# Conditional weights: masking, their layout and the counts' bank in a two-stage expert kernel on one Trainium2 core

## The chip, the cores and the metric

The kernel runs on one NeuronCore of one Trainium2 chip. The metric is device microseconds (us) of one execution. The kernel before took 288.45 us, the median of three runs (288.25 to 288.47).

## The reference, cut to what matters

Stage one (conditional weights): each of 128 batches mixes eight masked weight matrices with its own eight condition values, and its 32 tokens are multiplied by the mixed matrix. Stage two (experts): each batch takes the two experts with the largest condition values, and a shared MLP is added. Both stages are residual.

```python
masked_w = weight * mask[None, :, :]                     # weight (8, 128, 128), mask (128, 128)
w_bot = jnp.einsum('bg,got->bot', y, masked_w)           # y = cond_8 (128, 8)
x = x + jnp.einsum('bnt,bot->bno', x, w_bot) + bias      # x (128, 32, 128)

rw = jax.nn.softmax(cond_8); w, sel = jax.lax.top_k(rw, 2); w = w / w.sum(-1, keepdims=True)
# each selected expert e of batch b adds w * (gelu(x @ gate[e]) * (x @ up[e])) @ down[e]
# the shared MLP (128 -> 512 -> 128) adds the same form for every token
x = x + experts(x) + shared_mlp(x)
```

## The kernel before, in words

The features stand on the 128 partitions, the 4096 tokens (128 batches of 32) along the free axis, in eight tiles of 512 tokens (`x_sb`, `x1`, `acc`, `outT`). The order of all instructions is the order in which the program writes them: the scheduling is manual, and each engine runs its own list in that order. Waits follow from what is read and written, and from when a buffer of a pool comes free.

**Loads.** ScalarE's queue loads the condition (`cond_sb`, L86) and one half of the eight weight matrices; SyncE's queue loads the other half (L92), the mask (L94), two token tiles, the bias, the shared MLP and the other six token tiles. Expert weights follow on SyncE's queue once the routing knows the experts.

**Conditional weights.** `cond_rep` (L213) repeats each batch's eight values, TensorE transposes it into `ps_y` (L225), and `spread_cond` (L232) multiplies that by `own4`, a 0/1 pattern, into `yd`. After the transpose TensorE runs three idle products (`warm_up`, L130). The masked weights `mw` are made by four products (L248): for each half of the output features, VectorE does the first four matrices and GpSimd the other four. The output stands in the order (output feature, matrix), so an engine that runs over the features writes one value in every eight. `transpose_weights` (L256) transposes eight blocks of 128x128 on TensorE into four banks of PSUM, the first four blocks from the first half of `mw`, and ScalarE and VectorE copy them to `wT` (L269).

**Units.** A unit (`make_weights`, L279) makes the mixed weights of 32 batches for half of the output features: 16 matmuls into four banks (L286), then two copies on ScalarE and two on VectorE into `W` (L300, L302). There are eight units; three are made before the loop, and two in each of the first two rounds, one in the third. A round (L686) takes two token tiles: `apply_weights` (L305, tile `pz`, copied to `z` by ScalarE), then some routing steps (`advance`), then its units, then `finish_cond` (L324: four transposes to `pt`, and VectorE adds bias and residual into `x1`; GpSimd copies `x1` to `acc`).

**PSUM.** There are eight banks in three pools: three for tag `g`, three for `u`, two for `acc`. In stage one, `bank` (L274) goes through the pools in a fixed cycle, and so every further call of it moves all later tiles along that cycle. A tile takes a bank of its pool that is free, or waits for the readers of an older one.

**Routing.** `routing` (L357) is a chain of small VectorE instructions on the condition that ranks the experts, counts how many batches chose each (`ps_n`, two small matmuls), and assigns tiles of tokens to experts. It is cut in steps with `yield`; `advance(n)` first writes the matmuls that are due and then up to n steps, ending early at a `ROUND`. The counts' bank is drawn at L376 in the first round; its matmuls come at the start of the second round's `advance`, and the copy out of it (L405) comes in a later step, between that round's two units. The slots' matmuls (`ps_i`, `ps_w`, drawn at L487) end the chain, in the middle of the shared MLP.

**MLPs.** Expert and shared tiles run through one pipeline (L587): `pg` and `pu` products, gelu on ScalarE (L565), product on VectorE (L567), and one group later the down product `ps_out` (L552 for all). Two shared tiles run first, then 45 expert tiles with four sets of weight buffers, then the other shared tiles.

Of the kernel before, what the change touches and what calls it, by code (L numbers as in the profile page):

```python
# [10 lines left out]
F32 = mybir.dt.float32  # L11
# [19 lines left out]
def kernel(  # L31
# [16 lines left out]
    nc = tc.nc  # L48
# [38 lines left out]
    mask_sb = const.tile([P, P], F32, name="mask_sb")  # L87
    GQ = G // 2
    w0_sb = []
    for q, engine in enumerate((nc.sync, nc.scalar)):  # L90
        wq = const.tile([P, GQ, P], F32, name=f"w0_{q}", tag=f"w0_{q}")
        engine.dma_start(out=wq, in_=w0T[:, ts(q, GQ), :])  # L92
        w0_sb.append(wq)
    nc.sync.dma_start(out=mask_sb, in_=maskT)  # L94
    x_sb = []
# [32 lines left out]
    def warm_up(n):  # L128
# [5 lines left out]
    nc.scalar.activation(table, ones[:, 0:1], AF.Exp)  # L134

    R = P // G
    own = const.tile([P, R], F32, name="own")
    nc.gpsimd.affine_select(
        out=own,
        in_=ones[:, 0:R],  # L140
        pattern=[[-G, R]],
        base=0,
        channel_multiplier=1,
        compare_op=ALU.is_ge,
        fill=0.0,
    )
    nc.gpsimd.affine_select(
        out=own,
        in_=own,
        pattern=[[G, R]],  # L150
        base=G - 1,
        channel_multiplier=-1,
        compare_op=ALU.is_ge,
        fill=0.0,
    )

# [13 lines left out]
    for e in range(1, E):  # L170
# [34 lines left out]
    W = const.tile([P, B, P], F32, name="W")  # L205

    own4 = const.tile([P, OQ], F32, name="own4")
    nc.vector.tensor_reduce(
        own4, own.rearrange("p (j o) -> p o j", o=OQ), AX.X, ALU.add
    )  # L210

    cond_rep = const.tile([B, P // G, G], F32, name="cond_rep")
    nc.vector.tensor_copy(  # L213
        cond_rep, cond_sb.unsqueeze(1).to_broadcast([B, P // G, G])
    )
# [9 lines left out]
    nc.tensor.transpose(  # L225
        ps_y[:, 0:B], cond_rep.rearrange("b r g -> b (r g)"), ident
    )
# [15 lines left out]

    mw = const.tile([P, P, G], F32, name="mw")
    OH = QB * OB
    for half in range(P // OH):
        for q, engine in enumerate((nc.vector, nc.gpsimd)):
            engine.tensor_tensor(  # L248
                mw[:, ts(half, OH), ts(q, GQ)].rearrange("p o g -> p g o"),
                w0_sb[q][:, :, ts(half, OH)],  # L250
                mask_sb[:, ts(half, OH)].unsqueeze(1).to_broadcast([P, GQ, OH]),
                ALU.mult,
            )
    wT = const.tile([P, NQ, P], F32, name="wT")

    def transpose_weights():  # L256
        TQ = QB // 2
        for i in range(NQ // TQ):
            pool, tag = (ps_u, "u") if i % 2 else (ps_g, "g")
            pt = pool.tile([P, TQ * P], F32, name="pt", tag=tag)  # L260
            for k in range(TQ):
                q = i * TQ + k
                nc.tensor.transpose(  # L263
                    pt[:, ts(k, P)],
                    mw[:, ts(q, OB), :].rearrange("p o g -> p (o g)"),
                    ident,
                )
            copy = nc.vector.tensor_copy if i % 2 else nc.scalar.copy
            copy(wT[:, ts(i, TQ), :].rearrange("p q t -> p (q t)"), pt)  # L269
        spread_cond(NB, B - NB)  # L270
# [3 lines left out]
    def bank(name):  # L274

        pool, tag = {"g": (ps_g, "g"), "u": (ps_u, "u"), "o": (ps_o, "acc")}[next(ring)]
        return pool.tile([P, TB], F32, name=name, tag=tag)
# [66 lines left out]

    def tensor_later(*args, **kwargs):
        due.append((args, kwargs))

    def advance(n):

        for args, kwargs in due:  # L350
            nc.tensor.matmul(*args, **kwargs)  # L351
        due.clear()
        for _ in range(n):
            if next(steps, ROUND) is ROUND:
                break

    def routing():  # L357
# [17 lines left out]

        ps_n = bank("ps_n")  # L376
        tensor_later(ps_n[:, 0:E], ones_h, chosen, start=True, stop=True)
        tensor_later(ps_n[:, E : 2 * E], before_h, chosen, start=True, stop=True)
        ex_sum = small.tile([B, 1], F32, name="ex_sum")
# [23 lines left out]
        yield ROUND  # L403
        np_sb = small.tile([P, 2 * E], F32, name="np_sb")
        nc.vector.tensor_copy(np_sb, ps_n[:, 0 : 2 * E])  # L405
        of_expert, so_far = np_sb[:, 0:E], np_sb[:, E : 2 * E]
# [79 lines left out]

        ps_i = ps_g.tile([P, TB], F32, name="ps_i", tag="g")  # L487
        ps_w = ps_u.tile([P, TB], F32, name="ps_w", tag="u")
        for k in range(2):
# [17 lines left out]
            else:  # L507
# [5 lines left out]
                nc.vector.tensor_tensor(both_hot, hot, hot_0, ALU.add)  # L513
                tensor_later(ps_i[:, 0:NS], batch_h, both_hot, start=True, stop=True)
                tensor_later(ps_w[:, 0:NS], ones, hot_w, start=True, stop=True)
            yield
        yield ROUND

        for n, i, c, s in ((NE, 0, 0, S), (NE2, NE, NE * S, S2)):
# [166 lines left out]
    for i in range(LAST + 1):  # L686
# [4 lines left out]
        for _ in units[0:2]:  # L691
            weights()
            if i == 1:
                advance(1)
        if i == LAST:
# [109 lines left out]
```

## Time and profile before

| What | Value |
|---|---|
| median of three runs | 288.45 us |
| profiled execution, its own time | 288.74 us |
| its span, first to last instruction | 287.0 us |
| TensorE busy | 281.3 us, 98% |
| VectorE busy | 166.4 us, 58% |
| ScalarE busy | 79.0 us, 28% |
| GpSimd busy | 49.9 us, 17% |
| granted TensorE clock | 0.999 |
| DMA, mean over the span | 146 GB/s |

By stages of the span: 0 to 7.7 us are loads, set-up and the transposes of the weights (TensorE busy 6.11 us of 7.70); 7.7 to 35 us are the eight units and the four rounds (26.63 of 27.30); 35 to 50.4 us the first shared tiles (15.40 of 15.40); 50.4 to 220 us mostly the experts (169.60 of 169.60); the rest is the late shared tiles (63.58 of 67.00). Matmuls overlap in the records, so busy time counts a TensorE that has something in flight. A busy TensorE is not one at its peak, but where it has no gap, no other engine sets the time.

### The profile page before, as it was taken

To read this page: it belongs to the slowest core of one execution; us is meant where nothing else is said; L and a number is where in the kernel's file an instruction comes from. 1 tells how busy PE (TensorE), PEld (TensorE's weight loads), DVE (VectorE), ACT (ScalarE), POOL (GpSimd) and SP (SyncE) were. 2 spreads that over 40 slices of the span, in tenths; PEclk is the share of its full clock that TensorE was granted. 3 is DMA by queue.
4 is the path that set the end of the run, shared out by engine and by line. 5 is a ranking of instruction groups with operands and counts; after the bars stand their busy time and mean duration, and the time that the engine had idled before them with its cause. 6 is when DMAs were issued, how large, how long until landed. Compare 5 with 4: busy or idle time off the path is not lost.

```text
span 287.0 us, 12878 instructions
## 1 busy us (share of the span) xinstructions
PE 281.3 (98%) x5096; PEld 211.5 (74%) x5096; DVE 166.4 (58%) x473; ACT 79.0 (28%) x149; POOL 49.9 (17%) x289
## 2 busy tenths in 40 slices
PE   7999999999999999999999999999999999999995
PEld 6977644687788878888889999999997444444443
DVE  4889782366656566756665666666666432333232
ACT  5665322222222222222222222222222122221220
POOL 5002204122222122222222211312200000000000
PEclk9999999999999999999999999999999999999999
DMA  7800390266668667687667767777620200100001
GB/s 193 294 5 3 99 328 15 74 205 188 205 190 251 210 205 220 179 270 204 184 201 242 214 202 206 224 220 228 204 61 2 74 37 0 39 37 0 37 37 46
DMA packets 40770, 41.86 MB, mean 146 GB/s; under 512 B 2816, under 2 KB 26752, under 8 KB 40704
## 3 DMA queue, kind: packets, MB, share of 16 engines
q1 hardware_dynamic: 40272, 40.64, 46.3%
q8 instruction: 42, 0.69, 1.0%
q10 hardware_dynamic: 432, 0.33, 0.3%
q14 instruction: 24, 0.20, 0.2%
HBM read 38.87 MB, written 2.10 MB: 143 GB/s over the span
## 4 chain that ended last, share of the span: by engine, by line
PE 97%; DMA 1%; issue 0%; DVE 0%; ACT 0%
PE pg L552 30%; PE ps_out L552 29%; PE pu L552 29%; PE w L286 3%; PE pz L311 3%; PE pt L328 1%; DMA cond_sb<-in_cond_dram 1%; PE pt L263 1%; PE warm L130 0%; ACT W L302 0%; PE ps_w L351 0%; PE ps_y L225 0%; DVE o L622 0%; DVE cond_rep L213 0%; PE ps_n L351 0%
## 5 line engine op out<-in xcount | busy, mean ns | idle before, releaser
L567 DVE TENSOR_TENSOR h<-ge,pu 128x384 f32<-128x384 f32 (+1 forms) x117 | 69.3, 592 | 77.8 <-PE pu L552 77.7
L565 ACT ACTIVATE ge<-pg 128x384 f32<-128x384 f32 (+1 forms) x117 | 61.4, 525 | 187.2 <-PE pg L552 183.3
L662 DVE SCALAR_TENSOR_TENSOR acc<-ps_out,slot_w,acc 128x32 f32 x260 | 65.2, 251 | 30.0 <-DVE h L567 19.5
L552 PE MATMUL ps_out<-h,wd 128*32 128x192 f32 (+1 forms) x1440 | 74.2, 320 | 0.0
L552 PE MATMUL pg<-xg,wg 128*32 128x192 f32 (+1 forms) x1440 | 74.0, 320 | 0.0
L552 PE MATMUL pu<-xg,wu 128*32 128x192 f32 (+1 forms) x1440 | 73.9, 320 | 0.0
L657 POOL COPY xg<-x 128x32 f32 x260 | 42.0, 210 | 132.2 <-PE pu L552 122.5
L552 PEld LDWEIGHTS pg<-xg,wg 128*32 128x32 f32 x1440 | 50.8, 110 | 8.0 <-issue 1.7
L552 PEld LDWEIGHTS ps_out<-h,wd 128*32 128x32 f32 x1440 | 50.9, 110 | 7.2 <-DVE acc L662 0.8
L552 PEld LDWEIGHTS pu<-xg,wu 128*32 128x32 f32 x1440 | 51.0, 110 | 6.4
L552 PE MATMUL pg<-x,swg 128*128 128x512 f32 x64 | 33.0, 597 | 0.0
L552 PE MATMUL pu<-x,swu 128*128 128x512 f32 x64 | 32.7, 592 | 0.0
L552 PE MATMUL ps_out<-h,swd 128*128 128x512 f32 (+2 forms) x72 | 32.5, 546 | 0.0
L552 PEld LDWEIGHTS ps_out<-h,swd 128*128 128x128 f32 x72 | 13.3, 190 | 15.2 <-issue 13.5
L552 PEld LDWEIGHTS pu<-x,swu 128*128 128x128 f32 x64 | 12.2, 190 | 15.3 <-issue 15.1
L552 PEld LDWEIGHTS pg<-x,swg 128*128 128x128 f32 x64 | 11.7, 190 | 12.8 <-issue 12.0
L300 DVE COPY W<-w 128x512 f32<-128x512 f32 x16 | 10.1, 684 | 1.4 <-PE w L286 1.4
L286 PE MATMUL w<-yd,wT 32*128 32x128 f32 x256 | 10.1, 284 | 0.6 <-ACT W L302 0.5
L286 PEld LDWEIGHTS w<-yd,wT 32*128 32x128 f32 x256 | 8.9, 186 | 1.6 <-issue 0.7
L302 ACT COPY W<-w 128x512 f32<-128x512 f32 x16 | 8.5, 592 | 3.6 <-PE w L286 3.6
L333 POOL COPY acc<-x 128x512 f32<-128x512 f32 x6 | 3.7, 613 | 25.9 <-DVE x L329 25.8
L311 PE MATMUL pz<-W,xin 128*32 128x128 f32 x256 | 7.8, 274 | 0.1
(96 smaller groups left out, 70.0 us busy)
## 6 DMA issues: line engine op xcount, KB each, us to landing
wg<-in_gate_dram SPq DMA_DIRECT2D x45, 256.0 KB, 3.5
wu<-in_up_dram SPq DMA_DIRECT2D x45, 256.0 KB, 3.9
wd<-in_down_dram SPq DMA_DIRECT2D x45, 256.0 KB, 3.2
xin<-in_xT_dram SPq DMA_DIRECT2D x8, 256.0 KB, 5.5
out_dram<-o SPq DMA_DIRECT2D x5, 256.0 KB, 2.0
out_dram<-acc SPq DMA_DIRECT2D x2, 256.0 KB, 2.3
w<-in_w0T_dram SPq DMA_DIRECT2D x1, 256.0 KB, 2.9
w<-in_w0T_dram ACTq DMA_DIRECT2D x1, 256.0 KB, 3.5
```

Source lines behind the costliest of these rows:

```text
L263: nc.tensor.transpose(pt[:, ts(k, P)], mw[:, ts(q, OB), :].rearrange("p o g -> p (o g)"), ident,)
L286: nc.tensor.matmul(banks[j][:, ts(k, NB * OQ)], wT[rows, q0 + k, :], yd[rows, ts(i, NB), :].rearrange("p b o -> p (b o)"), start=True, sto ...
L300: nc.vector.tensor_copy(dst, src)
L302: nc.scalar.copy(dst, src)
L311: nc.tensor.matmul(pz[j * N : (j + 1) * N, ts(k, P)], x_sb[t][:, ts(b, N)], W[:, t * BT + b, :], start=True, stop=True,)
L328: nc.tensor.transpose(pt[:, ts(k, P)], z[:, ts(k, P)], ident)
L333: nc.gpsimd.tensor_copy(acc[:, ts(t, TB)], x1[:, ts(t, TB)])
L552: nc.tensor.matmul(out[rows], w[:, rows], x, **flags)
L565: nc.scalar.activation(ge[:, 0:n], pg[:, 0:n], AF.Gelu_apprx_tanh)
L567: nc.vector.tensor_tensor(h[:, 0:n], ge[:, 0:n], pu[:, 0:n], ALU.mult)
L657: nc.gpsimd.tensor_copy(xg[:, ts(j, N)], x1[:, bass.ds(v, N)])
L662: nc.vector.scalar_tensor_tensor(a, ps[:, ts(j, N)], slot_w[:, slot0 + j : slot0 + j + 1], a, ALU.mult, ALU.add,)
```

## The change

- The mask is issued first on SyncE's queue, ahead of its half of the weights. The condition was already first on ScalarE's queue and stays so. Both halves of the weights land in one tile, `w0_sb`.
- `own`, made by two GpSimd instructions, goes; `own4` is a reduction of the identity.
- `cond_rep`, `mw` and the rows of `wT` change their order from (output feature, matrix) to (group of four features, matrix, feature in the group).
- `mw` is made by two VectorE products of 512 columns, each half of the features and all eight matrices; GpSimd does none. Reads of the weights and the mask run over four values in a row, and the output is written in one run.
- The counts' bank is drawn when its matmuls are written, and is copied out directly behind them. This moves every later tile of the cycle by up to one place, and the copy stands ahead of the second round's routing steps on VectorE.
- The slots' banks are drawn when their matmuls are written, and copied out directly behind them.
- Two single routing steps of the second round, one behind each unit, go; the steps from the counts on move later, and end in the same place.

```diff
     mask_sb = const.tile([P, P], F32, name="mask_sb")
-    GQ = G // 2
-    w0_sb = []
+    nc.sync.dma_start(out=mask_sb, in_=maskT)
+    w0_sb = const.tile([P, G, P], F32, name="w0_sb")
     for q, engine in enumerate((nc.sync, nc.scalar)):
-        wq = const.tile([P, GQ, P], F32, name=f"w0_{q}", tag=f"w0_{q}")
-        engine.dma_start(out=wq, in_=w0T[:, ts(q, GQ), :])
-        w0_sb.append(wq)
-    nc.sync.dma_start(out=mask_sb, in_=maskT)
+        engine.dma_start(out=w0_sb[:, ts(q, G // 2), :], in_=w0T[:, ts(q, G // 2), :])
...
     nc.vector.tensor_reduce(
-        own4, own.rearrange("p (j o) -> p o j", o=OQ), AX.X, ALU.add
+        own4, ident.rearrange("p (r o) -> p o r", o=OQ), AX.X, ALU.add
     )
-    cond_rep = const.tile([B, P // G, G], F32, name="cond_rep")
+    cond_rep = const.tile([B, NJ, G, OQ], F32, name="cond_rep")
     nc.vector.tensor_copy(
-        cond_rep, cond_sb.unsqueeze(1).to_broadcast([B, P // G, G])
+        cond_rep, cond_sb.unsqueeze(1).unsqueeze(3).to_broadcast([B, NJ, G, OQ])
     )
...
-    mw = const.tile([P, P, G], F32, name="mw")
-    OH = QB * OB
-    for half in range(P // OH):
-        for q, engine in enumerate((nc.vector, nc.gpsimd)):
-            engine.tensor_tensor(
-                mw[:, ts(half, OH), ts(q, GQ)].rearrange("p o g -> p g o"),
-                w0_sb[q][:, :, ts(half, OH)],
-                mask_sb[:, ts(half, OH)].unsqueeze(1).to_broadcast([P, GQ, OH]),
-                ALU.mult,
-            )
+    NR = P // OQ
+    mw = const.tile([P, NR, G, OQ], F32, name="mw")
+    w0_r = w0_sb.rearrange("p g (r o) -> p r g o", o=OQ)
+    mask_r = mask_sb.rearrange("p (r o) -> p r o", o=OQ)
+    NRH = NR // 2
+    for half in range(2):
+        rows = ts(half, NRH)
+        nc.vector.tensor_tensor(
+            mw[:, rows, :, :],
+            w0_r[:, rows, :, :],
+            mask_r[:, rows, :].unsqueeze(2).to_broadcast([P, NRH, G, OQ]),
+            ALU.mult,
+        )
...
-        ps_n = bank("ps_n")
-        tensor_later(ps_n[:, 0:E], ones_h, chosen, start=True, stop=True)
-        tensor_later(ps_n[:, E : 2 * E], before_h, chosen, start=True, stop=True)
+        np_sb = small.tile([P, 2 * E], F32, name="np_sb")
+
+        def counts():
+            ps_n = bank("ps_n")
+            for k, rows in enumerate((ones_h, before_h)):
+                nc.tensor.matmul(ps_n[:, ts(k, E)], rows, chosen, start=True, stop=True)
+            nc.vector.tensor_copy(np_sb, ps_n[:, 0 : 2 * E])
+
+        due.append(counts)
...
         yield ROUND
-        np_sb = small.tile([P, 2 * E], F32, name="np_sb")
-        nc.vector.tensor_copy(np_sb, ps_n[:, 0 : 2 * E])
...
         for _ in units[0:2]:
             weights()
-            if i == 1:
-                advance(1)
```

More of the change, by code (lines that the diff above doesn't have):

```diff
@@ L134 @@
     nc.scalar.activation(table, ones[:, 0:1], AF.Exp)
[L136 to L145, printed above, removed]
-    )
[L147 to L155, printed above, removed]
     before = const.tile([P, P], F32, name="before")
@@ L225 @@
     nc.tensor.transpose(
-        ps_y[:, 0:B], cond_rep.rearrange("b r g -> b (r g)"), ident
+        ps_y[:, 0:B], cond_rep.rearrange("b j g o -> b (j g o)"), ident
     )
@@ L241 @@
     spread_cond(0, NB)
-    mw = const.tile([P, P, G], F32, name="mw")
-    OH = QB * OB
-    for half in range(P // OH):
-        for q, engine in enumerate((nc.vector, nc.gpsimd)):
-            engine.tensor_tensor(
-                mw[:, ts(half, OH), ts(q, GQ)].rearrange("p o g -> p g o"),
-                w0_sb[q][:, :, ts(half, OH)],
-                mask_sb[:, ts(half, OH)].unsqueeze(1).to_broadcast([P, GQ, OH]),
-                ALU.mult,
-            )
+    NR = P // OQ
[11 more added lines that the diff above has]
+        )
     wT = const.tile([P, NQ, P], F32, name="wT")
@@ L264, in transpose_weights @@
                     pt[:, ts(k, P)],
-                    mw[:, ts(q, OB), :].rearrange("p o g -> p (o g)"),
+                    mw[:, ts(q, NJ), :, :].rearrange("p j g o -> p (j g o)"),
                     ident,
@@ L343 @@
     due = []
-    def tensor_later(*args, **kwargs):
-        due.append((args, kwargs))
     def advance(n):
-        for args, kwargs in due:
-            nc.tensor.matmul(*args, **kwargs)
+        for matmuls in due:
+            matmuls()
         due.clear()
@@ L485, in routing @@
         yield
-        ps_i = ps_g.tile([P, TB], F32, name="ps_i", tag="g")
-        ps_w = ps_u.tile([P, TB], F32, name="ps_w", tag="u")
         for k in range(2):
@@ L513, in routing, with slots @@
                 nc.vector.tensor_tensor(both_hot, hot, hot_0, ALU.add)
-                tensor_later(ps_i[:, 0:NS], batch_h, both_hot, start=True, stop=True)
-                tensor_later(ps_w[:, 0:NS], ones, hot_w, start=True, stop=True)
+                due.append(lambda: slots(both_hot, hot_w))
             yield
         yield ROUND
+    def slots(both_hot, hot_w):
+        ps_i = ps_g.tile([P, TB], F32, name="ps_i", tag="g")
+        ps_w = ps_u.tile([P, TB], F32, name="ps_w", tag="u")
+        nc.tensor.matmul(ps_i[:, 0:NS], batch_h, both_hot, start=True, stop=True)
+        nc.tensor.matmul(ps_w[:, 0:NS], ones, hot_w, start=True, stop=True)
         for n, i, c, s in ((NE, 0, 0, S), (NE2, NE, NE * S, S2)):
```

## The prediction

> **What bounds the kernel now.** I read the page first. TensorE is busy for 281.3 of 287.0 us, so the question is where it has gaps that the change can reach; everything else is cover.
>
> ```profile
> span 287.0 us, 12878 instructions
> ...
> PE 281.3 (98%) x5096; PEld 211.5 (74%) x5096; DVE 166.4 (58%) x473; ACT 79.0 (28%) x149; POOL 49.9 (17%) x289
> ```
>
> Next the chain of work that ended last, for the first 34 us (start us, us, what). All that the diff touches lies here; from 26 us on the chain is TensorE without a break.
>
> ```profile
> 0.81 3.09 DMA cond_sb<-in_cond_dram
> ...
> 4.30 0.45 PE ps_y L225
> 4.75 1.28 PE warm L130 x6
> 6.03 0.10 issue
> 6.13 0.85 PE pt L263 x4
> 6.98 0.11 issue
> 7.09 0.63 PE pt L263 x4
> 7.72 3.66 PE w L286 x93
> ...
> 19.07 1.26 PE w L286 x31
> 20.33 0.57 ACT W L302
> 20.90 0.04 issue
> 20.95 1.17 PE w L286 x30
> ```
>
> Three places matter: 0.10 and 0.11 us of "issue" ahead of the two halves of the weights' transposes, and at 20.33 a gap of 0.57 + 0.04 us in which TensorE waits for a ScalarE copy into W. The timeline between 3.8 and 8.7 us (start us, us, engine, line) says what the first two are:
>
> ```profile
> 4.78 1.68 POOL L248 TENSOR_TENSOR mw<-w,mask_sb 128x256 f32<-128x256 f32 x2 [1.38 <-DMA w<-in_w0T_dram]
> 4.78 0.29 DVE L232 TENSOR_TENSOR yd<-ps_y,own 128x128 f32<-128x128 f32 x1 [0.37 <-PE ps_y L225]
> 4.99 1.95 DVE L248 TENSOR_TENSOR mw<-w,mask_sb 128x256 f32<-128x256 f32 x2
> ...
> 6.10 0.64 PEld L263 LDWEIGHTS pt<-ident,mw 128*128 128x128 f32 x4 [0.37 <-issue]
> ...
> 7.06 0.42 PEld L263 LDWEIGHTS pt<-ident,mw 128*128 128x128 f32 x4 [0.32 <-issue]
> ```
>
> The transposes' weights are loaded at 6.10 and 7.06. VectorE's two products into mw follow each other from 4.99, and the groups by tile give their lengths:
>
> ```profile
> L248 POOL TENSOR_TENSOR mw<-w,mask_sb x2: 732/864/997, 4.8 to 5.5; 128x256 f32<-128x256 f32 x2
> L248 DVE TENSOR_TENSOR mw<-w,mask_sb x2: 993/1050/1108, 5.0 to 5.8; 128x256 f32<-128x256 f32 x2
> ```
>
> The first, at 993 ns, ends at 4.99 + 0.99 = 5.98; the second at 4.99 + 1.95 = 6.94. Each weight load comes 0.12 us after such an end. GpSimd's pair ends at 4.78 + 1.68 = 6.46, earlier than VectorE's. So VectorE's products set both halves. The timeline from 18.5 us explains the third place:
>
> ```profile
> 18.86 0.18 PE L351 MATMUL ps_n<-chosen,ones_h 128*128 128x8 bf16 x1
> ...
> 20.31 1.07 ACT L302 COPY W<-w 128x512 f32<-128x512 f32 x2 [0.67 <-PE w L286]
> 20.35 1.29 DVE L300 COPY W<-w 128x512 f32<-128x512 f32 x2 [0.30 <-PE w L286]
> ...
> 20.95 1.17 PE L286 MATMUL w<-yd,wT 32*128 32x128 f32 x30 [0.45 <-ACT W L302]
> 21.56 0.17 DVE L405 COPY np_sb<-ps_n 128x16 f32<-128x16 f32 x1
> ```
>
> TensorE stops after the first matmul of unit six (two passes), and goes on 0.1 us after the first of ScalarE's two copies of unit five (1.07 us for two, so the first ends near 20.31 + 0.55 = 20.86). Counting the cycle of line 272: unit five takes two g banks, unit six wants a third, and that one holds the counts from 18.86 until the copy at 21.56. So unit six waits for the bank that unit five has just filled.
>
> **What the Trainium skill says.** "Vector Engine (DVE) Microarchitecture Reference", section "Measured stream behaviour on trn2 (trn3 not measured)": a port keeps its full rate, 1.054 ns a column, while its elements come in aligned runs of two or more adjacent words; an output stepping 24 words at every element costs 2.50. The trace agrees in kind: 256 columns that step 8 words take 993 and 1108 ns, whereas h, 512 columns in one run, takes about 0.68 us (28.99 in the timeline). "SBUF — State Buffer", section "Who interferes with whom": a VectorE instruction with two SBUF inputs contends with a GpSimd one that reads SBUF. Both engines run mw at once here, so part of the 993 ns may be that; no row separates the two. "DMA: Bandwidth & Descriptors", section "Issuing engines are not separate DMA queues": transfers of all queues interleave on the same 16 engines; the trace has both halves of the weights under way together, landing 2.9 and 3.5 us after issue.
>
> **The change, part by part.**
>
> Loads. SyncE issues w0 at 0.82 (0.39 us) and the mask at 1.26; swapped, the mask goes at 0.82 and w0 near 1.26. Landing times before, from the groups of the DMA issues: w0 0.82 + 2.9 = 3.7, mask 1.26 + 3.1 = 4.4, the ScalarE half 1.25 + 3.5 = 4.75. The bytes ahead of the token tiles are the same 580 KB, so I expect the last of the three near 4.75 again. VectorE is in yd until 5.07 and starts its next product at 4.99, which leaves 0.24 us. Now one product waits for all three transfers. Behind it in VectorE's list are only the wT copies, so a late transfer delays the transposes and nothing else. The condition stays first on its queue: 3.90, perhaps 0.1 to 0.2 less beside a smaller neighbour, perhaps 0.1 more; I take nothing. The later issues on SyncE's queue keep their places.
>
> own4. Two GpSimd instructions go (0.20 us each), and VectorE's reduction grows from 16 to 128 columns, about 0.3 us from near 1.4 us. VectorE then idles until 3.93 for the condition: nothing. If that cover were gone it would cost 0.1 us. cond_rep moves the same 128 columns; I keep 0.23 us, with 0.1 either way.
>
> mw. Two VectorE products of 512 columns, output in one run, inputs in runs of four words, no GpSimd beside them. No row shows this operation. From below: 0.68 us, the row of h. From above: the old price per column. Taking 0.15 us as fixed (0.68 less 512 x 1.04 ns), 256 columns at a mean of 1.05 us are 3.5 ns each, and 512 would take 1.95 us. I take 0.69, because all runs are four words or longer and the other reader is gone. Then the halves end at 4.99 + 0.69 = 5.68 and near 6.30 (copies of W follow each other every 0.61 us at 0.68 each).
>
> Transposes. Plus 0.12, the first weight load could be at 5.80 and the second half's at 6.42. TensorE is in the idle products until 6.03, and they become the bound. Eight transposes at 0.63 us for four end at 6.03 + 1.26 = 7.29 in place of 7.72: **0.43 us**. The first four took 0.85 before, after a pause; if that stays, 7.51 and 0.21 us. The wT copies still fit: the first unit needs ScalarE's first (near 6.9) and VectorE's first (near 7.2).
>
> Units one to five and the first round. TensorE and both copying engines move earlier together, since each copy waits for its own unit. The other banks drawn there came free long before (for unit five's first bank, the wait is for a copy of the unit before): nothing.
>
> Counts. Drawn at the start of the second round, the bank falls on the acc pool, and the copy right behind the matmuls releases it. In times of before, less the shift: the copy waits at 18.6 on VectorE until the counts are done at 19.07, and runs 19.17 to 19.34. Queued behind it is the weights' chain, rw to we, 1.49 us, now ending near 20.8; behind that, unit five's two copies, 20.8 to 22.1 in place of 20.35 to 21.6, and unit six's, 22.1 to 23.4. Unit six's four banks come from an x1 long done, from the two z copies (done 18.8 and 19.6) and from the counts' copy (19.4), all before 20.33. So the gap of **0.61 us** goes. What is late next: the round's pz needs unit five's copies (22.1) and TensorE reaches it at 20.33 + 1.17 + 1.02 = 22.5: 0.4 us of cover.
>
> Later steps. Without the two single steps, the counts' steps follow x1. VectorE still finishes unit seven's copies near 27.8, against 28.3 for the pz that reads them. The experts are known after the last x1, near 35 in place of 31.4, so SyncE's expert loads start some 3.5 us later: the twelve issues that began at 31.93 took 7.7 us and landed within 4, so all land by 47, and the first is needed at about 49.4 (50.40 less 1.0): nothing. The chain ends before the same matmuls, but with sixteen small steps in the last two gaps between products h. By the starts of their rows (36.1 to 40.9) that is 5.16 us from the first of these h to the end of both_hot. TensorE takes seven products of 0.86 us, 6.0, from the pu of that h to the slots' matmuls. Less 0.1 until h starts and 0.15 for a semaphore, 0.6 us of cover are left, 0.3 if GpSimd's acc copies hold two steps up.
>
> Sum: 0.43 + 0.61 = 1.04 us. Against the profiled execution: span 287.0 to 285.96, its own time 288.74 to 287.7. That execution is 0.29 above the median; I set the saving against the median: 288.45 - 1.04 = 287.41, and take **287.45**.
>
> **Rivals.**
>
> A: the start gives nothing, because a transfer lands near 5.6 or runs of four cost some 1.0 us a half; the gap still goes: 288.45 - 0.61 = 287.85. For it: no row shows the new form, and w0 is issued 0.44 us later. Against: 0.24 us of slack at either half.
>
> B: the gap comes back elsewhere. VectorE, 0.45 us later from the counts' copy on, is late for a pz, or the packed chain for the slots' matmuls. Its covers are 0.3 to 0.6 us; half of the gap lost leaves 288.45 - 0.43 - 0.3 = 287.7 to, with all of it, 288.05. For it: VectorE is busy for 23.4 of the 27.3 us of this stage.
>
> C: no change: the bank was not what unit six waited for, and mw's halves come out even: 288.45. Against: the place where TensorE stops, and the copy after which it goes on.
>
> D, slower: the price per column is the operation's own. Then halves of 1.95 us end at 4.99 + 3.8 = 8.8, the second half's transposes start at 8.9 in place of 7.09, and 1.8 - 0.6 = 1.2 us are lost: 289.65. It decides from 1.3 us a half on: 4.99 + 2.6 = 7.6 is 0.6 after the old 6.94, all that the bank gives. For it: VectorE takes over GpSimd's half, twice the columns. Against: h.
>
> **How the numbers follow.** Forecast 0.60 (287.2 to 287.75), A 0.15, B 0.13, C 0.05, D 0.07. What a measurement can tell from no change is about 0.2%, 0.58 us, so faster means under 287.87. Faster: nearly all of the forecast, half of A and a third of B: 0.58 + 0.08 + 0.04 = 0.70, less a little for covers that I could not see: 0.68. Slower: D and a tail of C: 0.08. Same: 0.24. The range 287.1 to 288.3 takes in the forecast, A and B, with the condition 0.2 us early at its lower end.
>
> **What would show it.** mw: two VectorE products near 0.69 us, ending by 6.3, and the eight transposes in one stretch ending near 7.3 (wrong: over 0.8 us, or a wait for a transfer). Bank: the gap ahead of unit six's second matmul gone, the counts' copy near 19. Cover: no wait of TensorE for VectorE at the pz of rounds three and four, and none ahead of the slots' matmuls; expert loads issued near 35 with no wait for them. The forecast is wrong if both parts show and the span is not near 286.0.

## The result and the profile after

The changed kernel takes 287.71 us, the median of 22 runs (286.98 to 289.85). Beside it on the same chip the kernel before took 288.52 us (22 runs, 288.22 to 289.54). The ratio is 0.9972, 95% interval 0.996 to 0.9984: 0.8 us saved, faster by 0.28%. A second comparison, after_again below, gives 1.2 us. The profiled execution took 286.98 us.

Span and busy time on the profile page of the changed kernel:

```profile
span 285.3 us, 12871 instructions
...
PE 280.1 (98%) x5096; PEld 199.3 (70%) x5096; DVE 166.3 (58%) x473; ACT 78.8 (28%) x149; POOL 48.1 (17%) x285
```

The span fell by 1.7 us, twice what the medians moved. One execution of before varies by 1.3 us and one of the changed kernel by 2.9 us; before's profiled run lay 0.2 us above its median here and the changed kernel's 0.7 us below. So the two profiles show where time moved, and the medians how much of it counts.

The chain of work that ended last in the changed kernel (start us, us, what):

```profile
1.25 3.96 DMA w_sb<-in_w0T_dram
...
5.29 0.70 DVE mw L229
...
6.04 1.33 PE pt L244 x8
7.38 3.66 PE w L267 x93
...
11.12 1.95 PE pz L292 x64
13.08 2.34 PE w L267 x64
15.42 1.02 PE pt L309 x8
...
18.46 2.12 PE w L267 x64
20.58 1.02 PE pt L309 x8
```

Three things are to be read in it. The chain now starts with the weights, which land at 5.21 us; before it started with the condition. The eight transposes are one piece of 1.33 us, and the first unit starts at 7.38 us instead of 7.72 (the chain begins a piece where the one before it ends; in TensorE's timeline, used below, the starts are 7.31 and 7.64). And the 64 matmuls from 18.46 us, units five and six (units are counted from zero here, as in the prediction), are one piece of 2.12 us, where before it was 1.26 + 0.57 + 0.04 + 1.17 = 3.04.

The changed kernel's products into mw, by tile:

```profile
L229 DVE TENSOR_TENSOR mw<-w_sb,mask_sb x2: 684/688/693, 5.3 to 5.9; 128x512 f32<-128x512 f32 x2
```

688 ns for 512 columns: the price that the prediction took (0.69), with VectorE alone. The timeline between 4.2 and 8.2 us shows what these products wait for, and who waits for them:

```profile
5.29 1.29 DVE L229 TENSOR_TENSOR mw<-w_sb,mask_sb 128x512 f32<-128x512 f32 x2 [0.69 <-DMA w_sb<-in_w0T_dram]
6.04 1.09 PEld L244 LDWEIGHTS pt<-ident,mw 128*128 128x128 f32 x8 [0.78 <-DVE mw L229]
```

They wait 0.69 us for a transfer of weights; the idle products end at 5.55 us, and the transposes' weight loads then wait for the first product. The timeline around the counts:

```profile
18.30 0.17 PE L359 MATMUL ps_n<-chosen,before_h 128*128 128x8 bf16 x1
...
18.50 0.17 DVE L360 COPY np_sb<-ps_n 128x16 f32<-128x16 f32 x1 [0.46 <-PE ps_n L359]
...
19.70 2.05 ACT L283 COPY W<-w 128x512 f32<-128x512 f32 x4 [0.67 <-PE w L267]
...
20.00 2.48 DVE L281 COPY W<-w 128x512 f32<-128x512 f32 x4
```

The counts leave their bank at 18.67, not at 21.73, and unit five's copies follow on both engines without TensorE waiting for them.

A table of the first stage, for all kernels of this document, comes from the starts in TensorE's timeline: when the first unit starts, how long each of two pairs of units takes (start of its first matmul to the start of the transposes behind it), when the first shared product pg starts, and when a certain transfer starts, which the trace's DMA records carry as an instruction transfer of 16 KB. The last column is the time from the first pg to the end of the span.

| kernel | first unit | units three and four | units five and six | first pg | instruction transfer | rest |
|---|---|---|---|---|---|---|
| before | 7.64 | 2.60 | 3.05 | 26.98 | 12.51 | 260.1 |
| changed | 7.31 | 2.34 | 2.11 | 25.45 | 11.81 | 259.8 |
| after_again (the changed kernel once more) | 7.19 | 2.56 | 2.00 | 25.44 | 11.84 | 259.8 |
| bank_alone | 7.58 | 3.01 | 2.00 | 26.27 | 12.63 | 259.8 |
| bank_steps_kept | 7.37 | 2.73 | 2.00 | 25.79 | 12.36 | 260.6 |
| mask_alone | 7.46 | 2.61 | 2.92 | 26.68 | 12.33 | 260.8 |
| after_weights_first | 6.84 | 2.61 | 2.00 | 25.13 | 11.73 | 260.0 |
| early_halves | 7.15 | 3.08 | 2.00 | 25.92 | 12.50 | 259.8 |
| early_halves, a second execution | 7.32 | 2.00 | 2.00 | 26.02 | 12.79 | 260.0 |
| old_layout_vector_only | 7.40 | 2.75 | 2.93 | 26.76 | 12.36 | 260.7 |
| new_layout_split | 8.74 | 2.00 | 2.00 | 27.17 | 12.46 | 260.4 |
| four_token_loads_fewer | 7.54 | 2.00 | 2.93 | 26.15 | 9.70 | 261.0 |
| bank_fewer_loads | 7.67 | 2.00 | 2.00 | 25.36 | 10.35 | 261.1 |
| weights_first_paced_loads | 6.88 | 2.00 | 2.00 | 24.69 | 9.97 | 260.1 |

From before to changed the first pg comes 1.53 us sooner: 0.33 from the start, 0.94 from units five and six, and 0.26 from units three and four, which the change wasn't seen to touch. A clean pair takes 2.00 us. The pair of units three and four became the question of the study. The rest differs by up to 1.3 us from one profile to another. That difference lies in stops among the expert tiles and the late shared tiles, which are not explained here. They are as large as what the change saves, so the columns of the first stage say more about a part of the change than the time of one execution does.

### The profile page after: what moved, and what is told of

The parts are those of the page before. It is cut to its first block, busy times and chain, and to the rows that moved or that the text cites. A ratio compares the mean times of both kernels' runs of the same rounds, so it can differ in the third digit from the quotient of the medians.

```text
span 285.3 us, 12871 instructions
## 1 busy us (share of the span) xinstructions
PE 280.1 (98%) x5096; PEld 199.3 (70%) x5096; DVE 166.3 (58%) x473; ACT 78.8 (28%) x149; POOL 48.1 (17%) x285
## 4 chain that ended last, share of the span: by engine, by line
PE 97%; DMA 1%; DVE 0%; ACTq 0%; issue 0%; DVEq 0%
PE pg L537 30%; PE ps_out L537 30%; PE pu L537 29%; PE w L267 3%; PE pz L292 3%; DMA w_sb<-in_w0T_dram 1%; PE pt L309 1%; PE pt L244 0%; DVE mw L229 0%; PE ps_w L502 0%; ACTq L86 0%; DVE o L607 0%; PE ps_n L359 0%; PE ps_i L501 0%; DVEq L229 0%
## 5 line engine op out<-in xcount | busy, mean ns | idle before, releaser
L537 PE MATMUL ps_out<-h,wd 128*32 128x192 f32 (+1 forms) x1440 | 72.0, 320 | 0.0
L537 PE MATMUL pg<-xg,wg 128*32 128x192 f32 (+1 forms) x1440 | 72.0, 320 | 0.0
L537 PE MATMUL pu<-xg,wu 128*32 128x192 f32 (+1 forms) x1440 | 72.0, 320 | 0.0
L537 PEld LDWEIGHTS pg<-xg,wg 128*32 128x32 f32 x1440 | 45.9, 110 | 11.8 <-issue 1.5
L537 PEld LDWEIGHTS ps_out<-h,wd 128*32 128x32 f32 x1440 | 45.9, 110 | 11.3 <-DVE acc L647 0.8
L537 PEld LDWEIGHTS pu<-xg,wu 128*32 128x32 f32 x1440 | 46.1, 110 | 10.3
L537 PEld LDWEIGHTS pg<-x,swg 128*128 128x128 f32 x64 | 11.7, 190 | 12.8 <-issue 12.0
L267 PE MATMUL w<-yd,wT 32*128 32x128 f32 x256 | 9.5, 283 | 0.0
```

The lines of the kernel that those rows point to most:

```text
L267: nc.tensor.matmul(banks[j][:, ts(k, NB * OQ)], wT[rows, q0 + k, :], yd[rows, ts(i, NB), :].rearrange("p b o -> p (b o)"), start=True, sto ...
L537: nc.tensor.matmul(out[rows], w[:, rows], x, **flags)
```

## The experiments

### The two parts alone, and the whole again

`bank_alone` is before with only the routing part: the counts' and slots' banks drawn and emptied at their matmuls, and the two single steps gone. `mask_alone` is before with only the loads, the layout and the masking. `after_again` is the changed kernel unaltered.

```diff
# bank_alone, against before
-        ps_n = bank("ps_n")
-        tensor_later(ps_n[:, 0:E], ones_h, chosen, start=True, stop=True)
-        tensor_later(ps_n[:, E : 2 * E], before_h, chosen, start=True, stop=True)
+        def counts():
+            ps_n = bank("ps_n")
...
+        due.append(counts)
...
-            if i == 1:
-                advance(1)
```

> The kernel before with the routing part of the change alone: counts' and slots' banks drawn and copied at their matmuls, two single routing steps gone; loads, layout and mw as before. My theory, after the two traces: the gap ahead of the second matmul of unit six goes, with the refill of TensorE behind it, so units five and six take near 2.1 us instead of 3.0; the first unit starts at 7.7 as before. 0.6 to 0.9 us faster than before (ratio 0.997 to 0.998). Rival, all of the gain comes from the start of the kernel: same time as before. Rival, the bank's stall is only moved to a wait of TensorE for VectorE: under 0.3 us.

> The kernel before with the loads, the layout and mw on VectorE alone; the routing and its banks as before. My theory: the first unit starts 0.2 to 0.4 us sooner, at 7.3 to 7.5 in place of 7.72, set by the landing of the weights; the gap at unit six stays. 0.1 to 0.4 us faster than before (ratio 0.9986 to 0.9997). Rival, the start gives nothing in most executions because the weights land late: ratio 1.000 or above, with a wider spread than before. Rival, it gives all: 0.8 us.

> The changed kernel unaltered, as a second profile and for comparison on the same chip with its two parts. If the parts add up: the sum of both alone. The span of its profile shows what varies: by my theory the landing of the weights on which the first mw waits (5.29 in the first profile), and with it the start of the first unit; from there to the first expert tile 41.6 us as in the first profile. Rival, the spread is in the later stages: the first unit starts at 7.4 again and the expert stage differs.

Measured against the same runs of before (288.92 us, 30 runs):

| kernel | median us (runs) | ratio, 95% interval |
|---|---|---|
| bank_alone | 287.73 (11) | 0.9963, 0.9949 to 0.9976 |
| mask_alone | 288.92 (14) | 0.9996, 0.9978 to 1.0014 |
| after_again | 287.74 (12) | 0.9958, 0.9945 to 0.997 |

The routing part alone gives what the whole gives, and more than the 0.6 to 0.9 us expected of it. The start alone gives nothing that can be told from zero, but its interval reaches from 0.6 us faster to 0.4 slower and so holds both the forecast 0.43 us and nothing. In its profile the first pg comes 0.30 us sooner than in before, and the rest takes 0.8 us longer. The chain of mask_alone shows the gap still in its place, at 20.03 us:

```profile
1.25 4.19 DMA w_sb<-in_w0T_dram
...
5.52 0.70 DVE mw L229
...
14.54 0.14 issue
...
18.89 1.14 PE w L267 x32
20.03 0.57 ACT W L283
20.60 0.04 issue
20.64 1.17 PE w L267 x30
```

and that of bank_alone shows it gone, from 19.40 us, with another one in the round before:

```profile
13.35 1.31 PE w L286 x34
14.65 0.54 issue
15.19 1.17 PE w L286 x30
...
19.40 2.00 PE w L286 x64
```

So the counts' bank is what stopped unit six (the two steps that went with it are looked at next; the slots' banks, also in bank_alone, belong to matmuls near 40 us, far behind the gap). And it costs more than the named wait: the pair takes 2.92, 2.93, 2.93 and 3.05 us with it and 2.00 without. The records of single matmuls show where most of that comes from. One lasts 0.27 us, but in a stream of them one starts every 0.03 us (64 in 2.00 us). At the gap of before 0.72 us pass between two starts, 20.23 and 20.95 us, and the stream behind it loses another 0.1 us before it is as dense as ahead of it.

### Do the two removed steps matter?

`bank_steps_kept` puts the two single steps back into bank_alone.

```diff
         for _ in units[0:2]:
             weights()
+            if i == 1:
+                advance(1)
```

> The kernel before with the counts' and slots' banks drawn and copied at their matmuls, and nothing else: the two single routing steps of the second round stay. My theory, that the bank alone is what pays: units five and six in 2.0 us, as with the steps gone, and 0.9 to 1.2 us faster than before (ratio 0.996 to 0.997). Rival, the steps that were in VectorE's way between the units' copies pay too: less than half of that.

288.26 us (22 runs, 287.52 to 289.74), ratio 0.9979, 0.9967 to 0.9991, against 288.74 us (50 runs). Units five and six take 2.00 us: for the gap, the bank is enough, and the two steps don't matter. The time saved is 0.6 us, less than the 0.9 to 1.2 expected. The ratio lies outside bank_alone's interval, though the two intervals overlap. In the profile the first pg comes 0.5 us sooner than in bank_alone and the rest takes 0.7 us longer; whether the steps have a part in that stays open.

### What made one masking product slow?

`old_layout_vector_only` leaves before as it is and moves GpSimd's two products to VectorE. `new_layout_split` is the changed kernel with four matrices on VectorE and four on GpSimd.

```diff
# old_layout_vector_only, against before
-        for q, engine in enumerate((nc.vector, nc.gpsimd)):
+        for q, engine in enumerate((nc.vector, nc.vector)):
```

> The kernel before with GpSimd's two products of mw given to VectorE, in the old order of features and matrices: four products of 256 columns, each writing one word in eight, and no GpSimd beside them. If the stepping output sets the price (runs of four are what pays): near 0.8 to 1.05 us each, 3.2 to 4.2 us in all, and the first unit starts near 9.5, 2 us slower than before. If GpSimd's reading beside it was the price: near 0.42 us each, the price of 256 columns in one run, and the time is that of before or less.

> The changed kernel with the masking split between VectorE and GpSimd again, in the new layout: four matrices and 256 columns for each product, two products an engine. Theory that two engines with two SBUF inputs each slow one another whatever the layout: one of the two pays 0.35 to 0.5 us more a product than alone; VectorE alone would be 0.15 + 256 x 1.05 ns = 0.42 us, so 0.8 to 0.9 where it loses and 0.42 to 0.5 where GpSimd does. Rival, only the stepping output suffers: VectorE at 0.42 and GpSimd under 0.7 us in both halves. In either case the second half is ready no earlier than the changed kernel's (6.68 us) by more than 0.3 us.

The groups of mw, first of old_layout_vector_only:

```profile
L248 DVE TENSOR_TENSOR mw<-w,mask_sb x4: 611/629/642, 4.7 to 6.1; 128x256 f32<-128x256 f32 x4
```

then of new_layout_split:

```profile
L230 DVE TENSOR_TENSOR mw<-w_sb,mask_sb x2: 425/646/867, 5.9 to 6.2; 128x256 f32<-128x256 f32 x2
L230 POOL TENSOR_TENSOR mw<-w_sb,mask_sb x2: 701/762/822, 6.1 to 6.7; 128x256 f32<-128x256 f32 x2
```

| 256 columns on VectorE | alone | GpSimd beside it |
|---|---|---|
| output stepping 8 words | 611 to 642 ns | 993 and 1108 (before), 617 and 1119 (bank_alone) |
| output in one run | near 420 (estimate: 150 + 256 x 1.05) | 425 and 867 |

Both theories were half right. In either layout the two engines hold each other up: a VectorE product that loses to GpSimd's takes 0.4 to 0.5 us more. Which one loses is not fixed: in bank_alone VectorE's first product kept its 617 ns and GpSimd's two took 987 and 1072, where GpSimd's first in before took 732. And stepping costs something as well: an estimate from these rows is (629 - 150) / 256 = 1.9 ns a column, with the 0.15 us of the prediction as fixed part, against 1.05 in one run. My expectation for old_layout_vector_only, 0.42 us by the one theory or over 3.2 us for the four by the other, missed on both sides: its four products took 2.01 us.

That is no more than the two engines needed together. The masking of bank_steps_kept, which is that of before, and of old_layout_vector_only:

```profile
4.71 2.03 POOL L248 TENSOR_TENSOR mw<-w,mask_sb 128x256 f32<-128x256 f32 x2 [1.30 <-DMA w<-in_w0T_dram]
4.72 1.56 DVE L248 TENSOR_TENSOR mw<-w,mask_sb 128x256 f32<-128x256 f32 x2
```

```profile
4.75 2.01 DVE L248 TENSOR_TENSOR mw<-w,mask_sb 128x256 f32<-128x256 f32 x4
```

In the old layout, then, the masking takes 2.0 us with GpSimd's help or without it. In the new layout VectorE alone takes 1.29, and the two engines together took 1.70 (new_layout_split, 5.86 to 7.56 us). So the shorter masking takes both, the new layout and VectorE alone. That the first unit of old_layout_vector_only starts at 7.40 us, nearly as early as in the changed kernel, comes from an earlier start: its first product needs one half of the weights and began at 4.75 us, where the changed kernel's waited for both halves until 5.29. With the masking of before, the first unit starts anywhere between 7.37 and 7.67 us in the five profiles of the table that have it. Its one time was 289.17 us, beside 288.92 for before.

new_layout_split took 289.32 us in one execution, beside 288.74 for before, and started its first unit at 8.74 us. Its weights landed 0.6 us later than in the changed kernel, so that TensorE stood still between its idle products and the transposes:

```profile
4.07 1.49 PE L127 MATMUL warm<-ones 128*128 128x128 f32 x6
...
6.84 1.97 PE L245 MATMUL pt<-ident,mw 128*128 128x128 f32 x8 [1.28 <-POOL mw L230]
```

The eight transposes took 1.97 us (421 ns a matmul, 273 in most of the others) and the three units behind them 4.56 instead of 3.82. It is tempting to put that down to the 1.28 us of idling, but early_halves, below, idles 1.25 us at the same place and most of its transposes take 273 ns. In every profile the early 128-column matmuls of TensorE take 421 ns, those of this kernel ahead of its idling too, and later ones 273. The switch came between 4.1 and 6.6 us in the other thirteen profiles and near 10.2 us in this one; the granted clock reads 1.00 on both sides of it. Whether the idling put it off here is not shown.

### The order of the loads

The mask now goes ahead of SyncE's half of the weights. `after_weights_first` issues that half first again; the rest is the changed kernel.

```diff
-    nc.sync.dma_start(out=mask_sb, in_=maskT)
     w0_sb = const.tile([P, G, P], F32, name="w0_sb")
     for q, engine in enumerate((nc.sync, nc.scalar)):
         engine.dma_start(out=w0_sb[:, ts(q, G // 2), :], in_=w0T[:, ts(q, G // 2), :])
+    nc.sync.dma_start(out=mask_sb, in_=maskT)
```

> The changed kernel with SyncE's half of the weights issued ahead of the mask again. My theory, that the swap only trades the condition's landing for the weights': condition back from 3.0 to about 3.9, the last of the weights from 5.2 back to about 4.75, the transposes still near 6.0 and the first unit near 7.3, held now by the idle products. Time within 0.2 us of the changed kernel's (ratio to before 0.996). Rival, the swap costs what mw's shorter products gain: 0.3 us faster than the changed kernel.

Its chain:

```profile
4.90 0.70 DVE mw L229
...
5.65 1.26 PE pt L244 x8
6.91 3.66 PE w L267 x93
...
12.61 1.31 PE w L267 x35
13.91 0.14 issue
```

The masking starts at 4.90 us and the first unit at 6.84, 0.35 to 0.47 us sooner than in the two executions of the changed kernel, and well ahead of the 7.3 us expected. The condition lands 0.8 us later, and the chain now runs through it: the masking starts right behind yd, which waits for it. The median is 287.68 us (13 runs), ratio 0.9967, 0.9952 to 0.9982: the same time as the changed kernel's within the noise. In the table units three and four took 2.61 us, so that their pair ends only 0.2 and 0.3 us sooner (15.15 us against 15.35 and 15.45). The first pg comes 0.3 us sooner, which is too little for these intervals to show.

`early_halves` goes further: the weights come in the order (half, group, matrix, feature), each queue brings one half, the weights go ahead of the mask, the first masking product goes ahead of yd, and the three idle products are left out.

```diff
-    w0_sb = const.tile([P, G, P], F32, name="w0_sb")
+    w0_sb = const.tile([P, P // 4, G, 4], F32, name="w0_sb")
...
-    warm_up(3)
```

> The changed kernel with the weights laid out in HBM in the new order, each queue loading one half of the output features (so that the first mw product needs one transfer and the mask), weights ahead of the mask, the first mw product ahead of yd on VectorE, and the three idle products of TensorE ahead of the transposes left out. By my theory the first half of mw starts near 4.4, the second ends near 5.95, and the first unit starts near 6.7 in place of 7.2 to 7.3: 0.5 us faster than the changed kernel (ratio to before 0.994 to 0.995). Rival, instruction fetch or the cold clock takes it back: the first unit starts sooner, but a gap of issue grows ahead of unit four: no gain.

287.91 us (22 runs), ratio 0.9967, 0.9955 to 0.9979. The first half of the masking waited for the mask, now last on its queue (3.65 us to landing), and the first unit started at 7.15 instead of the 6.7 expected. Units three and four took 3.08 us: of the 0.49 us that this start gains on before, the pair loses 0.48, which is what the expectation's rival said. A second execution of the same kernel had TensorE's granted clock at 0.50 from 8 to 11 us, so that its first three units took 4.83 us instead of 3.82; with TensorE that late, units three and four took 2.00.

### What holds up units three and four?

Within units three and four the chain has a wait that it calls "issue": nothing that the profile shows was missing. In most kernels it lies behind the 34th or 35th of the 64 recorded matmuls of the pair, ahead of unit four's second matmul (each matmul is recorded as two passes). In the changed kernel it is too short for the chain to name: 0.14 us pass between two starts at that place. In early_halves it lies behind the 41st:

```profile
12.85 1.49 PE L266 MATMUL w<-yd,wT 32*128 32x128 f32 x41
15.05 0.95 PE L266 MATMUL w<-yd,wT 32*128 32x128 f32 x23 [0.71 <-issue]
```

Six recorded matmuls fewer run ahead of the pair in that kernel (its `warm_up(3)` is gone), and the stop has moved back by six or seven. Counted in the traces it is one place in TensorE's own list: in all nine profiles that stop, 449 recorded instructions of TensorE (matmuls, weight loads and waits) lie ahead of it. And there the next matmul starts 2.33 to 2.56 us after the start of the instruction transfer (14.86 - 12.51 = 2.35 in before, 14.25 - 11.81 = 2.44 in the changed kernel, 14.06 - 11.73 = 2.33 in after_weights_first), while the first unit starts anywhere from 6.84 to 7.64. The five profiles without a stop come to that matmul 2.47 to 4.55 us after the transfer's start. The section "Instruction fetch mechanics" of "Runtime: NRT & Kernel Launch" in the Trainium skill says that an engine's instructions are streamed in by DMA in blocks of 16 KiB, mostly hidden. The size agrees, and so does a stop at a fixed place of TensorE's list; if this is such a block, it is not hidden here. While TensorE comes to this place the token tiles fill the DMA engines. Two kernels leave out the loads of the last four token tiles and use the first four in their stead, so that they compute on other input:

```diff
-    for t in range(EARLY, NTILE):
+    for t in range(EARLY, NTILE // 2):
         load_x(t)
+    x_sb += x_sb
```

> The kernel before without the loads of the last four token tiles; the first four stand in for them, so that part of the input is left out. It asks what the gap of issue ahead of unit four's second matmul is (0.13 to 0.54 us in five profiles, a 16 KB instruction transfer ending shortly before it). If that transfer is slowed or started late beside the token loads: the gap goes, and the transfer starts earlier than 12.3 us. If it is not: the gap stays at 0.1 to 0.5 us. The gap of 0.6 us at unit six stays either way.

> The routing part alone (bank_alone) without the loads of the last four token tiles: the first four tiles stand in for them, so the result is that of other input. Theory: the 0.54 us in which TensorE waits for nothing visible ahead of unit four's second matmul is a late fetch of instructions, a 16 KB transfer that shares the DMA engines with the token tiles and started at 12.63 us; with fewer tiles it starts before 11 us, the gap is gone, and the stretch from the first unit to the first shared product is 18.70 - 0.54 = 18.2 us or less. Rival: the pause belongs to that place of the program, whatever is loaded: 0.5 us again and 18.7.

The timeline of TensorE, first in bank_alone:

```profile
13.28 1.38 PE L286 MATMUL w<-yd,wT 32*128 32x128 f32 x34
15.19 1.17 PE L286 MATMUL w<-yd,wT 32*128 32x128 f32 x30 [0.54 <-issue]
16.29 1.09 PE L328 MATMUL pt<-ident,z 128*128 128x128 f32 x8
```

then in bank_fewer_loads:

```profile
13.37 2.07 PE L287 MATMUL w<-yd,wT 32*128 32x128 f32 x64
15.37 1.09 PE L329 MATMUL pt<-ident,z 128*128 128x128 f32 x8
```

The transfer starts at 10.35 us, the 0.54 us are gone, and the pair takes 2.00 instead of 3.01; from the first unit to the first pg it is 17.69 us instead of 18.69. four_token_loads_fewer, the same edit on before, also has its pair at 2.00, and keeps the bank's gap. Both expectations held. Their times, 288.16 and 288.81 us in one execution each, say nothing on this: their rest is the longest of the table. A third run meant to do this to early_halves (its label early_halves_fewer_loads) carried early_halves unaltered by mistake; it is the second execution told of above, and its expectation was not tested.

That the loads make the pause is shown by these pairs, of one execution for each kernel, and by the version below. That the instruction transfer is the link, and that it is TensorE's, is inferred: no view names the engine that it feeds, but the stop has a fixed place in TensorE's list and a fixed distance from that transfer.

### A version that doesn't run into it

`weights_first_paced_loads` is after_weights_first with the last four token tiles asked for later. GpSimd writes one column of the tile from a finished unit's W, and so the load, which overwrites it, waits for that unit (`LATE` gives the token tile for each unit). Nothing is left out.

```diff
+    def load_x_behind(t, unit):
+        xt = const.tile([P, TB], F32, name=f"xin{t}", tag=f"xin{t}")
+        row, col = unit // 2 * NB, unit % 2 * QB * OB
+        nc.gpsimd.tensor_copy(xt[:, 0:1], W[:, row, col : col + 1])
+        nc.sync.dma_start(out=xt, in_=xT[:, ts(t, TB)])
+        x_sb.append(xt)
+
+    LATE = {2: 4, 4: 5, 5: 6, 6: 7}
...
         next(unit)
         next(unit)
+        k = B // NB * 2 - len(units) - 1
+        if k in LATE:
+            load_x_behind(LATE[k], k)
```

> The kernel of after_weights_first with the last four token tiles asked for later: each is loaded behind the copies of a unit (tile 4 behind unit two, 5 behind four, 6 behind five, 7 behind six, counted from zero), so that TensorE's instructions are fetched beside fewer loads. Nothing is left out. Theory, the pair of units in the first round ends some 3.5 us after the fetch starts whatever came before it: here the fetch starts near 10.4 us as in bank_fewer_loads, units three and four take 2.00 us instead of 2.61, the first shared product comes near 6.84 + 17.69 = 24.5 us, the median is 287.68 - 0.6 = 287.1 us. Rival, the fetch follows TensorE's own progress, not the loads: it starts near 11.7 us again, 2.6 us for the pair, median 287.7. Second rival, a later fetch now meets the late loads: the pause moves to units five and six, and the median is 287.5 to 287.7.

286.9 us (6 runs, 286.49 to 287.02), ratio 0.9926, 0.9911 to 0.9942, against 288.7 us (11 runs). It beats both kernels: 2.1 us under before. Its chain:

```profile
5.80 1.14 PE pt L253 x8
6.95 3.66 PE w L276 x93
...
12.65 2.00 PE w L276 x64
14.64 1.03 PE pt L318 x8
...
17.69 2.00 PE w L276 x64
...
20.71 0.05 issue
```

No "issue" within units three and four; both pairs take 2.00 us, and the first pg starts at 24.69, 2.3 us sooner than in before. In the view of the DMA queues over the first 20 us the load of the engines (tenths of their time, 0.5 us each) lasts until 12.5 us in the changed kernel:

```profile
DMA  0001987999999799999999999410000001000000
GB/s 0 0 0 40 144 197 225 373 352 303 377 250 181 279 356 341 329 330 361 385 393 389 402 414 348 160 41 20 0 0 0 0 0 33 0 0 0 0 0 0
```

and in weights_first_paced_loads it breaks off near 10 us and comes in pieces after 12:

```profile
DMA  0006598999995999999600004841000006820010
GB/s 0 0 0 61 124 334 243 386 343 365 295 148 180 356 353 357 384 380 356 217 8 0 0 0 74 283 164 37 0 0 0 0 0 123 295 107 0 0 33 0
```

The expectation held in place and sign: transfer at 9.97 instead of near 10.4, first pg 24.7 instead of 24.5. The median fell by more than the 0.6 us of the pair, about 1.2 by the two ratios (0.9967 less 0.9926, of 288.7; each is uncertain by some 0.4 us). Its six runs lie within 0.5 us of one another, those of after_weights_first within 2.1. This fits a pause that is longer in some executions than in the profiled one; it was not looked at further.

## Why the prediction was right, and where it was wrong

The time (287.71 measured, 287.45 forecast, in a range of 287.1 to 288.3), the sign and the mechanism of the larger part held. The total is closer than its parts: of the 1.04 us forecast, 0.8 were measured (1.2 in after_again), with the bank worth more than its term and the start's term not seen in the times.

**The bank, 0.61 us: right mechanism, too small.** Unit six waited for the bank that unit five had filled, because the counts held the third; the gap goes when the counts leave early, and comes back nowhere. The term that was mis-sized is the wait itself: I priced it at what the chain names, 0.57 + 0.04. The pair shrank by 0.94 us (3.05 to 2.11), and by 1.05 to the clean 2.00. The rest is the stream of matmuls that breaks off and starts again.

**The masking, 0.69 us a half: right.** 684 and 693 ns. Of the two bounds, h was the nearer, and rival D is out: its upper price took the 993 ns for the operation's own, and by old_layout_vector_only (611 to 642 ns) some 0.4 us of that was GpSimd.

**The loads: wrong.** The step was "the bytes ahead of the token tiles are the same 580 KB, so I expect the last of the three near 4.75 again", and for the condition "I take nothing". Changed order moved both: the condition was used from 3.00 us instead of 3.93, the last weights landed at 5.21 instead of 4.75 (5.44 in mask_alone). One product now waits for all three transfers, so the masking started at 5.29 instead of 4.99, and the 0.24 us of slack was used up. The idle products, which I had as the bound at 6.03, ended near 5.55 because they follow the condition. The transposes started at 6.04, as forecast, by luck: two errors cancelled. The first unit came 0.34 us earlier by the chain, not 0.43. (The pause that I gave as the reason for before's slow first transposes is not it: they took 447 and 388 ns because TensorE's matmuls were then still at their first length, 421 ns. The changed kernel's took 474 and 407, which is the 0.07 us by which eight exceed the forecast 1.26.)

**"TensorE and both copying engines move earlier together ... nothing": incomplete.** Not all of the unit stage follows the first unit. Within units three and four TensorE waits until 2.3 to 2.6 us after the start of the instruction transfer, and an earlier start gets through only as far as that transfer is earlier too. In early_halves it was not, and 0.48 of 0.49 us were lost there. In the changed kernel it happened to start 0.7 us sooner than in before, and the pair even gained 0.26 us. The chain of before had the sign of it, 0.13 us of "issue" at 14.73, in a line that I passed over; the pair lost 0.60 us by it. Rival A, "the start gives nothing", is wrong in its mechanism, since the products were as fast as forecast; its time is not decided, because the interval of mask_alone holds 0.43 us as well as nothing.

With all token loads in place the transfer started at 11.7 to 11.8 us in three profiles (changed, after_again, after_weights_first) and at 12.3 to 12.8 in the other eight, among them new_layout_split, which has both parts of the change too. What sets that start stays open.

**The covers held.** No stop of TensorE at the pz of rounds three and four; ps_i started at 40.42, 0.55 us behind both_hot's end at 39.87, with no piece of another engine in the chain there; the expert loads began at 34.49 us and no expert product waited for them. Rival B, the gap coming back elsewhere, is out by that (its upper end, with all of the gap lost, is 288.45 - 0.43 = 288.02, not 288.05); C by bank_alone.

## What to carry to other kernels

A wait that the chain names can be well below what its removal gives: where it cuts a stream of short matmuls, measure the stretch around it against a clean one (3.05 against 2.00 us here, for a wait of 0.61). An earlier start is worth only what the next fixed point lets through, so look for a place that doesn't move when the start does. Pieces of "issue" with everything at hand are candidates: count the engine's own instructions up to them in two kernels, and if the count is the same, the place belongs to its list and not to the work. Loads that nobody needs yet may be what stands behind such a stop. Issue them when they are needed: four token tiles asked for 6 to 13 us later were worth about 1.2 us, as much as the whole change.

## What the runs showed of the hardware

- With 3.5 MB of loads queued in the first 14 us, TensorE stopped near 14.5 us in nine of eleven profiles, always behind 449 recorded instructions of its own and until 2.33 to 2.56 us after the start of a 16 KB instruction transfer. The named stop was up to 0.7 us, the cost 0.3 to 1.1. With 1 MB of the loads gone or later, the transfer started at 9.7 to 10.4 us instead of 11.7 to 12.8, and TensorE did not stop.
- VectorE and GpSimd, each with a product of two SBUF inputs, hold each other up in either layout: 256 stepping columns took VectorE 611 to 642 ns alone and 993 to 1119 where it lost to GpSimd; where GpSimd lost, it took 987 and 1072. The two together were no faster than VectorE alone (2.03 and 2.01 us).
- An output that steps 8 words costs about 1.9 ns a column on VectorE and an output in one run 1.05 (estimates from 629 ns for 256 columns and 688 for 512, with 0.15 us as fixed part).
- A load of 4 KB landed 2.0 to 2.2 us after issue when the other queue's first transfer was the 64 KB mask, and 2.9 to 3.1 when that was 256 KB of weights; the last weights took 3.9 to 4.7 us in the first case and, in the same form of load, 3.4 to 3.6 in the second.
- TensorE's early 128-column matmuls took 421 ns in every profile and later ones 273, with a switch between 4.1 and 6.6 us, in one profile near 10.2, while the granted clock read 1.00.
